# Moving the rows that GpSimd multiplies to other element offsets, and giving it 15 of 32 products

## The chip, the cores and the metric

The kernel runs on one core of one Trainium2 chip, in float32. The metric is device time in microseconds (us), the median of several executions; a separate execution was recorded by the profiler. Engines are called PE (TensorE, matmul), DVE (VectorE), ACT (ScalarE), POOL (GpSimd) and SP (SyncE, which issues the DMAs here).

## The reference, cut to what matters

The model is a conv and attention block, a position term, a Mamba stack, and a token-mixing and expert tail. The change touches only the Mamba stack: two images of 3136 tokens and 256 channels, six layers, inner width 512, 16 states per inner channel. Cut to the part around the change:

```python
def step(h, inp):
    u_t, dt_t, B_t, C_t = inp
    h = jnp.exp(dt_t[..., None] * A) * h + (dt_t * u_t)[..., None] * B_t[:, None, :]
    y_t = jnp.einsum('bds,bs->bd', h, C_t)
    return (h, y_t)
...
x_dbl = uc @ xp_w
dt_r = x_dbl[..., :DT_RANK]
Bm = x_dbl[..., DT_RANK:DT_RANK + D_STATE]
Cm = x_dbl[..., DT_RANK + D_STATE:]
dt = jax.nn.softplus(dt_r @ dt_w + dt_b)
y = selective_scan(uc, dt, A, Bm, Cm, Dp)
y = y * jax.nn.silu(z)
return y @ out_w
```

So for each inner channel and each state, a linear recurrence over the tokens: a decay exp(dt A), an input dt u B, and a product of the state with C that is summed over the 16 states.

## The kernel before, in words

The kernel has three phases in a row: `conv_phase`, `mamba_phase`, `tail_phase`. In `mamba_phase` the tokens are cut into 7 chunks of T = 448. With 2 images and 6 layers this gives 84 chunks, numbered j. The recurrence of a chunk is done in 32 scans, numbered s (i = 32 j + s over the whole phase). `order` lists them: k, one of four blocks of 128 inner channels; ng, one of four groups of states; pr, which half of the block's channels. The 128 partitions of a scan hold 32 channels for each of 4 states, and its free dimension holds two rows (g = 0, 1) of 448 tokens, for two more groups of 32 channels.

For each scan i there are these steps, each a function of its own:

- `inputs(i)`: ACT copies the kept state into element 0 of both rows of a tile x (449 elements a row). Then POOL multiplies dtur (dt u, repeated over the states) with bc row ng (B), into elements 1 to 448 (L824). The tile x comes from a pool of nine.
- `decays(i)`: ACT makes exp(dt A) in a PSUM tile da (L807, two instructions), from dtr. There are three da tiles.
- `scan(i)`: DVE runs the recurrence over 898 elements (L844). If s is in `on_pool`, it writes to x, otherwise over da, and in that case DVE at once makes the product with C (bc row 4 + ng) into x (L837 on DVE).
- `keep(i)`: ACT copies each row's last state out (L833).
- `pool_product(i)`: for s in `on_pool`, POOL makes the product with C in place in x (L837 on POOL).
- `gather(i)`, for odd i: PE sums the states of two scans into the PSUM tile acc (L859) and so frees their two x tiles. `gate(i)`, after each 8 scans: DVE multiplies acc with silu(z) (L869).
- `fetch(i)`, at the first scan of a block: SP loads the next block's dtr and dtur from DRAM (`repeat`, 8 DMAs, L781); there are two tiles of each.

B and C come from `x_keep(j)`: its result is stored to DRAM and loaded back, repeated over 32 partitions, as bc (8 rows of T elements, L625). dt and dt u come from `dt_keep`, `dt_softplus` and `dt_out(j, d)`. The last stores dt's block d, makes dtu = dt u on POOL (L652), and stores that. These and the other steps (`u_project` to `z_silu`) prepare chunk j + 1 while chunk j is scanned. The `n_` steps are the norm for chunk j + 2, and the `y_` steps the output projection of chunk j - 1.

The program is written out by hand in one order: every step is put at a place, in units of scans, all are sorted by place, and each engine runs its own instructions in that order. `places` holds the places of the preparing steps within a chunk, `first` and `last` those of steps that only some chunks have, and the loop over i those of the scan's own steps. A place fixes an order in an engine's queue, not a time; the waits between engines do the rest.

Where rows start matters to the change. Elements are counted from the start of a tile: before, bc's rows lie 448 apart, from 0; dt's and hz's rows 448 apart, from 0; dtur's rows 449 apart, from 1; the rows of x that are multiplied start at 1 and 450.

Of the kernel before, what the change touches and what calls it, by code (L numbers as in the profile page):

```python
# [10 lines left out]
F32 = mybir.dt.float32  # L11
# [7 lines left out]
P = 128  # L19
# [13 lines left out]
NB = DI // P  # L33
# [17 lines left out]
def chunk(c, n=NT):  # L51
    return slice(c * n, (c + 1) * n)
# [409 lines left out]
def mamba_phase(ctx: ExitStack, tc: tile.TileContext, I, t1_d, t2_d):  # L462
# [87 lines left out]

    M = {"dt": cp.tile([P, NB, T], F32, name="dt")}
    us = [cp.tile([P, T + 3], F32, name=f"u{n}") for n in range(2)]
    hzs = [cp.tile([P, 2 * NB, T], F32, name=f"hz{n}") for n in range(2)]
    dtus = [cp.tile([P, T], F32, name=f"dtu{n}") for n in range(2)]
# [13 lines left out]
    def u_keep(j, d):  # L570
        tail = layer_of(j + 1)["tail"][:, d, :]
        u = M["u", d] = us[d % 2]
        nc.scalar.copy(u[:, 0:3], tail)
        nc.scalar.copy(u[:, 3:], M["mm"])  # L574
        nc.scalar.copy(tail, u[:, T:])

    def u_convolve(j, d):
        ps = M["mm"] = mm()[:, :T]
        for k in range(4):
            nc.tensor.matmul(  # L580
                ps, lhsT=layer_of(j + 1)["w_cv"][:, 4 * d + k, :], rhs=M["u", d][:, k : k + T],
                start=(k == 0), stop=(k == 3),
            )
# [33 lines left out]
    def x_keep(j):  # L617

        xd = M["xd"] = one.tile([DTR + 2 * DS, T], F32, name="xd")
        nc.scalar.copy(xd, M["mm"])  # L620
        bc_d = dp.tile([2 * DS, T], F32, name="bc_d")
        nc.sync.dma_start(bc_d, xd[DTR:, :])
        bc = QS[j + 1]["bc"] = two.tile([P, 8, T], F32, name="bc")
        for n in range(4):
            nc.sync.dma_start(  # L625
                bc[chunk(n, HD)],
                bc_d.rearrange("(m n) t -> n m t", n=4)[n].unsqueeze(0).to_broadcast([HD, 8, T]),
            )
        QS[j + 1]["dt_d"], QS[j + 1]["dtu_d"] = {}, {}
# [26 lines left out]
    def dt_back(j):  # L656
        repeat(QS[j + 1], 0)
# [117 lines left out]
    def repeat(Q, k):  # L775

        dtr = dtrs[k % 2]
        dtur = two.tile([P, 4, T + 1], F32, name="dtur")[:, :, 1:]
        for t, src in ((dtr[:, :, 1:], Q["dt_d"]), (dtur, Q["dtu_d"])):
            for n in range(4):  # L780
                nc.sync.dma_start(t[chunk(n, HD)], src[k].rearrange("(g p) t -> p g t", p=HD))  # L781
        Q[k] = dtr, dtur
# [2 lines left out]
    order = [(k, ng, pr) for k in range(NB) for ng in range(4) for pr in range(2)]  # L785
    ns = len(order)

    on_pool = (2, 3, 5, 7, 8, 9, 10, 15, 19, 21, 22, 26)
    chunks = [(b, layer, c) for b in range(B) for layer in range(NL) for c in range(MCH)]
    layers, QS, X, D, acc = {}, {}, {}, {}, {}  # L790

    def layer_of(j):
        return layers[chunks[j][:2]]
# [80 lines left out]
    def fetch(i):  # L874
        repeat(QS[i // ns], i % ns // 8 + 1)
# [15 lines left out]
    def load_rest(j):  # L891
# [3 lines left out]


    places = {
        (u_project, 0): 1.304, (u_keep, 0): 2.607, (z_project, 0): 3.501, (z_keep, 0): 3.952,
        (u_project, 1): 4.609, (u_keep, 1): 5.234, (y_project, 1): 6.869, (y_add, 1): 7.331,
        (y_project, 0): 7.461, (y_add, 0): 9.223, (u_convolve, 0): 10.048, (u_add, 0): 10.687,  # L900
        (u_project, 2): 10.964, (u_keep, 2): 11.995, (u_convolve, 1): 12.277, (u_add, 1): 13.134,
        (u_convolve, 2): 14.792, (u_add, 2): 15.184, (u_project, 3): 15.393, (u_keep, 3): 16.616,
        (u_convolve, 3): 17.440, (u_add, 3): 17.991, (z_project, 1): 18.040, (u_silu,): 18.479,
        (z_keep, 1): 18.732, (x_project,): 19.334, (x_keep,): 20.167, (dt_project, 2): 20.825,
        (dt_keep, 2): 21.601, (dt_project, 0): 21.808, (dt_keep, 0): 22.204,
        (dt_project, 1): 23.295, (dt_keep, 1): 23.374, (dt_project, 3): 24.269,
        (dt_keep, 3): 24.913, (dt_softplus,): 24.942, (dt_out, 0): 25.013, (dt_back,): 25.337,
        (z_project, 2): 25.840, (dt_out, 1): 26.057, (z_keep, 2): 26.747, (z_project, 3): 27.262,
        (load,): 27.272, (dt_out, 2): 27.694, (z_keep, 3): 28.791, (n_squares,): 29.547,
        (n_root,): 29.821, (n_invert,): 31.105, (n_spread,): 32.629, (n_weighted,): 32.761,  # L910
        (load_rest,): 34.587, (dt_out, 3): 36.194, (z_silu,): 38.909,
    }
    first = {
        f_load: 12.141, f_mean: 23.145, f_center: 23.266, f_squares: 23.712, s_root: 23.835,
        s_invert: 24.267, s_spread: 25.138, f_scale: 25.476,
    }
    last = {
        l_squares: 0.000, s_root: 0.000, s_invert: 1.571, s_spread: 2.712, l_weighted: 3.271,
# [5 lines left out]
    def put(place, what, *args):  # L924
        events.append((place, len(events), what, args))
# [7 lines left out]
            put(j * ns + place, what, j)  # L933

    for i in range(n):
        put(i - 1.652, inputs, i)
        put(i - 1.217, decays, i)
        put(i + 0.4, scan, i)
        put(i + 1.080, keep, i)
        if i % ns in on_pool:  # L940
            put(i + 2.886, pool_product, i)
        if i % 2 == 1:
            put(i + 3.900, gather, i)
        if i % 8 == 7:
            put(i + 4.422, gate, i)
        if i % 8 == 0 and i % ns < ns - 8:
            put(i + 1.264, fetch, i)
    for j in range(-2, nj + 1):
        for (what, *args), place in places.items():
            target = {"y": j - 1, "n": j + 2, "l": j + 2}.get(what.__name__[0], j + 1)  # L950
# [559 lines left out]
```

## Time and profile before

| what | value |
|---|---|
| median of 3 runs | 10932.15 us (10929.53 to 10943.57) |
| the profiled execution's own time | 10941.86 us |
| its span | 10940.1 us |
| busy share of the span: PE, DVE, ACT, POOL | 82%, 88%, 70%, 81% |
| scans on DVE (L844) | 1680 into da, 1008 into x |
| products with C (L837) | 1680 on DVE, 1008 on POOL |
| inputs on POOL (L824) | 2688 |
| dt u on POOL (L652) | 336 |

The three runs lie within 14 us of each other. The page gives, for each group of equal instructions, its line, engine, operation, what it writes and reads, how many there are, then the busy time in us and the mean of one in ns, and then the idle time of that engine just before them with what ended most of it. The Mamba phase is the even middle part of the span, from about 1770 to 9600 us.

### The profile page before, as it was taken

Reading aid. Unit: us, or ns where it says so; the run is one execution under the profiler, and the core shown is the slowest. Engines: PE = TensorE matmul, PEld = TensorE weight load, DVE = VectorE, ACT = ScalarE, POOL = GpSimd, SP = SyncE. Lnnn points to the kernel's source line nnn. Section 1 sums busy time; section 2 is a strip of 40 time slices with the busy share of each in tenths; the row PEclk is TensorE's granted clock in tenths of the full one; section 3 lists DMA queues with packets and bytes.
Section 4 is the critical chain, followed back from the end, with each engine's and each line's share of the span. In section 5 each row is a group of like instructions: output and inputs, shape, how many; then the busy total and the mean of one; then the engine's idle time right before and its main releaser. Section 6 shows DMA issues by size and latency. Waiting matters only on the chain. (4 is left out here: it accounts for less than half of the span.)

```text
span 10940.1 us, 121750 instructions
## 1 busy us (share of the span) xinstructions
PE 9002.0 (82%) x39394; PEld 3541.5 (32%) x39394; DVE 9666.1 (88%) x7545; ACT 7671.5 (70%) x15776; POOL 8900.7 (81%) x5268
## 2 busy tenths in 40 slices
PE   8999997777777777777777777777777777789999
PEld 3333323323322222222332222222222222245555
DVE  6998996999999999999999999999999999967453
ACT  4664665777787777777787777778777777743343
POOL 5887996898899999999999999999999999911110
PEclk9999997888888888888888888888888888789999
DMA  1000004555555555555555555555555555511111
GB/s 48 16 16 11 16 11 97 123 128 123 117 130 120 128 121 125 120 122 128 134 140 122 127 122 122 128 121 129 121 122 123 120 125 122 127 51 31 40 40 40
DMA packets 674228, 1068.88 MB, mean 98 GB/s; under 512 B 83082, under 2 KB 668050, under 8 KB 672722
## 3 DMA queue, kind: packets, MB, share of 16 engines
q1 hardware_dynamic: 673586, 1061.09, 41.4%
q8 instruction: 309, 5.06, 0.2%
q14 instruction: 333, 2.73, 0.1%
HBM read 875.91 MB, written 184.91 MB: 97 GB/s over the span
## 5 line engine op out<-in xcount | busy, mean ns | idle before, releaser
L824 POOL TENSOR_TENSOR x<-dtur,bc 128x896 f32<-128x896 f32 x2688 | 5132.3, 1933 | 63.3 <-PE acc L859 54.5
L844 DVE TENSOR_TENSOR_SCAN da<-da,x 128x898 f32<-128x898 f32 x1680 | 3398.0, 2023 | 210.6 <-POOL x L824 145.1
L807 ACT ACTIVATE da<-dtr,am 128x449 f32<-128x449 f32 x5376 | 3428.7, 638 | 188.5 <-DVE x L844 96.6
L562 PE MATMUL mm<-xn,w_in 128*128 128x448 f32 x2656 | 1482.3, 691 | 706.9 <-ACT hz L603 238.6
L844 DVE TENSOR_TENSOR_SCAN x<-da,x 128x898 f32<-128x898 f32 x1008 | 2002.4, 2013 | 1.7 <-POOL x L824 0.9
L837 POOL TENSOR_TENSOR x<-x,bc 128x896 f32<-128x896 f32 x1008 | 1947.9, 1932 | 25.5 <-ACT state L833 17.5
L837 DVE TENSOR_TENSOR x<-da,bc 128x896 f32<-128x896 f32 x1680 | 1834.5, 1092 | 82.5 <-DVE da L844 1.8
L859 PE MATMUL acc<-x,sum_w 128*32 128x448 f32 x10752 | 1584.7, 664 | 35.6 <-POOL x L837 30.0
L335 POOL TENSOR_TENSOR pr<-kr,qo 128x980 f32<-128x980 f32 (+1 forms) x672 | 1149.0, 1722 | 196.7 <-PE pa L368 186.7
L580 PE MATMUL mm<-u,w_cv 128*128 128x448 f32 x2656 | 1089.3, 552 | 174.9 <-ACT u L574 158.2
L562 PEld LDWEIGHTS mm<-xn,w_in 128*128 128x128 f32 x2656 | 551.0, 230 | 1676.2 <-issue 733.6
L833 ACT COPY state<-da 128x2 f32<-128x2 f32 x1680 | 264.0, 157 | 1079.0 <-DVE x L837 1068.9
L360 PE MATMUL pa<-onehot,rel 49*64 49x490 f32 (+5 forms) x7168 | 834.0, 558 | 114.1 <-DVE av L377 111.4
L377 DVE TENSOR_TENSOR av<-pa,vr 128x980 f32<-128x980 f32 (+1 forms) x672 | 740.2, 1101 | 115.0 <-PE pa L368 84.9
L380 DVE TENSOR_REDUCE qo<-av 128x20 f32<-128x980 f32 (+1 forms) x672 | 743.3, 1106 | 41.4 <-DVE av L377 1.0
L309 ACT COPY vr<-vt 128x2500 f32<-128x2500 f32 (+14 forms) x296 | 468.6, 1614 | 424.6 <-DVE av L377 424.4
L580 PEld LDWEIGHTS mm<-u,w_cv 128*128 128x128 f32 x2656 | 477.3, 189 | 801.3 <-issue 372.0
L652 POOL TENSOR_TENSOR dtu<-dt,hz 128x448 f32<-128x448 f32 x336 | 382.6, 1139 | 420.3 <-ACT state L833 356.7
L368 PE MATMUL pa<-pr,hmat 64*64 64x490 f32 (+1 forms) x5376 | 641.6, 546 | 0.0
L633 PE MATMUL mm<-xd,w_dt 16*128 16x448 f32 x664 | 480.3, 814 | 186.5 <-ACT xd L620 111.1
L708 PE MATMUL mm<-hz,w_out 128*128 128x448 f32 x1344 | 553.3, 555 | 78.3 <-DVE res L715 47.4
L859 PEld LDWEIGHTS acc<-x,sum_w 128*32 128x32 f32 x10752 | 232.0, 117 | 1021.6 <-issue 819.7
(209 smaller groups left out, 11038.1 us busy)
## 6 DMA issues: line engine op xcount, KB each, us to landing
dtr<-dt_d SPq DMA_DIRECT2D x1344, 224.0 KB
dtur<-dtu_d SPq DMA_DIRECT2D x1344, 224.0 KB
bc<-bc_d SPq DMA_DIRECT2D x336, 448.0 KB
dt_d<-dt SPq DMA_DIRECT2D x336, 224.0 KB
dtu_d<-dtu SPq DMA_DIRECT2D x336, 224.0 KB
cb<-comb_d SPq DMA_DIRECT2D x128, 196.0 KB
t<-t_d SPq DMA_DIRECT2D x28, 448.0 KB
w_in<-in_in_w SPq DMA_DIRECT2D x12, 1024.0 KB
```

Source lines behind the costliest of these rows:

```text
L335: nc.gpsimd.tensor_tensor(pr[:, :, :m].rearrange("p f (q k) -> p f q k", k=KK), K[n][:, :, at : at + m].rearrange("p f (q k) -> p f q k", ...
L360: nc.tensor.matmul(pa[chunk(f, 64), g, :m], lhsT=rel[64 * g : 64 * g + rows, bh, kind, f, :], rhs=onehot[64 * g : 64 * g + rows, col : col ...
L368: nc.tensor.matmul(pa[chunk(f, 64), g, :m], lhsT=hmat[chunk(g, 64), :], rhs=pr[chunk(g, 64), f, :m], start=False, stop=True, tile_position ...
L377: nc.vector.tensor_tensor(av[:, :, :m], PA.pop(i)[:, :, :m], V[n][:, :, at : at + m], ALU.mult)
L380: nc.vector.tensor_reduce(qo[:, :, h * HW + w : h * HW + w + nq], av[:, :, :m].rearrange("p f (q k) -> p f q k", k=KK), AX.X, ALU.add,)
L562: nc.tensor.matmul(ps, lhsT=layer_of(j + 1)["w_in"][:, k, chunk(at, P)], rhs=Q["xn"][:, k, :], start=(k == 0), stop=(k == 1),)
L580: nc.tensor.matmul(ps, lhsT=layer_of(j + 1)["w_cv"][:, 4 * d + k, :], rhs=M["u", d][:, k : k + T], start=(k == 0), stop=(k == 3),)
L807: nc.scalar.activation(D[i][:, chunk(g, T + 1)], dtr[:, 2 * pr + g, :], AF.Exp, scale=L["am"][:, col : col + 1],)
L824: nc.gpsimd.tensor_tensor(x[:, :, 1:], Q[k][1][:, 2 * pr : 2 * pr + 2, :], wide(Q["bc"][:, ng, :]), ALU.mult)
L837: engine.tensor_tensor(both(X[i])[:, :, 1:], both(h)[:, :, 1:], wide(QS[j]["bc"][:, 4 + ng, :]), ALU.mult)
L844: nc.vector.tensor_tensor_scan(h, D[i], X[i], 0.0, ALU.mult, ALU.add)
L859: nc.tensor.matmul(acc[0][chunk(g, HD), :T], lhsT=sum_w, rhs=both(X[i - 1 + g // 2])[:, g % 2, 1:], start=False, stop=(ng == 3), tile_posi ...
```

## The change

The rows of bc, dt and dtur become four elements longer than T where they were T or T + 1, and the part in use begins at element 3 (bc, dt) or 1 (dtur). bc's and dt's rows then start at 3 plus a multiple of 452, dtur's at 1 plus a multiple of 452; x and hz stay as they are. The list `on_pool` grows from 12 to 15 scans of 32, and its members are others. All numbers in `places`, `first` and the loop over i are new; `last` stays.

```diff
-    M = {"dt": cp.tile([P, NB, T], F32, name="dt")}
+    M = {"dt": cp.tile([P, NB, T + 4], F32, name="dt")[:, :, 3 : T + 3]}
...
-        bc = QS[j + 1]["bc"] = two.tile([P, 8, T], F32, name="bc")
+        bc = QS[j + 1]["bc"] = two.tile([P, 8, T + 4], F32, name="bc")[:, :, 3 : T + 3]
...
-        dtur = two.tile([P, 4, T + 1], F32, name="dtur")[:, :, 1:]
+        dtur = two.tile([P, 4, T + 4], F32, name="dtur")[:, :, 1 : T + 1]
...
-    on_pool = (2, 3, 5, 7, 8, 9, 10, 15, 19, 21, 22, 26)
+    on_pool = (0, 1, 2, 5, 6, 11, 12, 13, 18, 19, 20, 21, 26, 27, 29)
...
     places = {
-        (u_project, 0): 1.304, (u_keep, 0): 2.607, (z_project, 0): 3.501, (z_keep, 0): 3.952,
...
-        (dt_keep, 3): 24.913, (dt_softplus,): 24.942, (dt_out, 0): 25.013, (dt_back,): 25.337,
...
-        (load_rest,): 34.587, (dt_out, 3): 36.194, (z_silu,): 38.909,
+        (z_project, 1): -2.539, (z_keep, 1): -2.072, (z_project, 0): -1.532, (z_keep, 0): -1.505,
...
+        (n_squares,): 15.411, (u_silu,): 16.174, (n_root,): 16.174, (n_invert,): 18.591,
...
+        (dt_softplus,): 23.997, (dt_out, 0): 24.128, (z_project, 2): 25.470, (dt_back,): 25.963,
+        (z_keep, 2): 26.109, (z_project, 3): 26.637, (load,): 26.647, (dt_out, 1): 26.808,
+        (z_keep, 3): 27.219, (z_silu,): 27.439, (dt_out, 2): 27.869, (n_spread,): 28.232,
+        (n_weighted,): 28.912, (load_rest,): 31.780, (dt_out, 3): 44.121,
     }
...
     for i in range(n):
-        put(i - 1.652, inputs, i)
-        put(i - 1.217, decays, i)
+        put(i - 3.160, inputs, i)
+        put(i - 1.850, decays, i)
         put(i + 0.4, scan, i)
-        put(i + 1.080, keep, i)
+        put(i + 0.410, keep, i)
         if i % ns in on_pool:
-            put(i + 2.886, pool_product, i)
+            put(i + 0.951, pool_product, i)
         if i % 2 == 1:
-            put(i + 3.900, gather, i)
+            put(i + 3.316, gather, i)
         if i % 8 == 7:
-            put(i + 4.422, gate, i)
+            put(i + 4.228, gate, i)
         if i % 8 == 0 and i % ns < ns - 8:
-            put(i + 1.264, fetch, i)
+            put(i + 0.050, fetch, i)
```

More of the change, by code (lines that the diff above doesn't have):

```diff
@@ L897, in mamba_phase @@
     places = {
-        (u_project, 0): 1.304, (u_keep, 0): 2.607, (z_project, 0): 3.501, (z_keep, 0): 3.952,
[L899 to L903, printed above, removed]
@@ L904, in mamba_phase @@
-        (z_keep, 1): 18.732, (x_project,): 19.334, (x_keep,): 20.167, (dt_project, 2): 20.825,
-        (dt_keep, 2): 21.601, (dt_project, 0): 21.808, (dt_keep, 0): 22.204,
-        (dt_project, 1): 23.295, (dt_keep, 1): 23.374, (dt_project, 3): 24.269,
-        (dt_keep, 3): 24.913, (dt_softplus,): 24.942, (dt_out, 0): 25.013, (dt_back,): 25.337,
-        (z_project, 2): 25.840, (dt_out, 1): 26.057, (z_keep, 2): 26.747, (z_project, 3): 27.262,
-        (load,): 27.272, (dt_out, 2): 27.694, (z_keep, 3): 28.791, (n_squares,): 29.547,
@@ L910, in mamba_phase @@
-        (n_root,): 29.821, (n_invert,): 31.105, (n_spread,): 32.629, (n_weighted,): 32.761,
-        (load_rest,): 34.587, (dt_out, 3): 36.194, (z_silu,): 38.909,
+        (z_project, 1): -2.539, (z_keep, 1): -2.072, (z_project, 0): -1.532, (z_keep, 0): -1.505,
+        (u_project, 0): -1.249, (u_keep, 0): -0.200, (u_project, 1): 1.151, (u_keep, 1): 1.663,
+        (y_project, 0): 4.063, (y_add, 0): 5.160, (y_project, 1): 5.762, (y_add, 1): 6.434,
+        (u_convolve, 0): 7.637, (u_add, 0): 7.892, (u_convolve, 1): 8.295, (u_add, 1): 8.658,
@@ new lines, in mamba_phase @@
+        (u_project, 3): 9.800, (u_keep, 3): 10.138, (u_project, 2): 11.100, (u_keep, 2): 11.358,
+        (u_convolve, 3): 13.166, (u_add, 3): 14.088, (u_convolve, 2): 14.814, (u_add, 2): 15.199,
+        (n_squares,): 15.411, (u_silu,): 16.174, (n_root,): 16.174, (n_invert,): 18.591,
+        (x_project,): 19.692, (x_keep,): 19.881, (dt_project, 0): 20.231, (dt_keep, 0): 20.575,
+        (dt_project, 2): 21.356, (dt_keep, 2): 21.523, (dt_project, 3): 22.720,
+        (dt_keep, 3): 23.054, (dt_project, 1): 23.113, (dt_keep, 1): 23.784,
@@ L912, in mamba_phase @@
+        (dt_softplus,): 23.997, (dt_out, 0): 24.128, (z_project, 2): 25.470, (dt_back,): 25.963,
+        (z_keep, 2): 26.109, (z_project, 3): 26.637, (load,): 26.647, (dt_out, 1): 26.808,
+        (z_keep, 3): 27.219, (z_silu,): 27.439, (dt_out, 2): 27.869, (n_spread,): 28.232,
+        (n_weighted,): 28.912, (load_rest,): 31.780, (dt_out, 3): 44.121,
     }
     first = {
-        f_load: 12.141, f_mean: 23.145, f_center: 23.266, f_squares: 23.712, s_root: 23.835,
-        s_invert: 24.267, s_spread: 25.138, f_scale: 25.476,
+        f_load: 2.954, f_mean: 5.165, f_center: 5.401, f_squares: 6.561, s_root: 7.195,
@@ L916, in mamba_phase @@
+        s_invert: 9.457, s_spread: 10.252, f_scale: 10.610,
     }
```

## The prediction, made before the changed kernel was run

> **What bounds the kernel now.** The page's slices came first: from about 1770 to 9600 us VectorE and GpSimd both stand at 9 tenths, TensorE at 7. This is the Mamba stage, 84 chunks of 32 scans; nothing outside it is edited. I then asked for the busy times of an even stretch (columns: length, busy time and count of PE, PEld, DVE, ACT, POOL, then clock, DMA share, GB/s):
>
> ```profile
> 2650.00:9200.00 6550.00, 5130.30 (x18392) 1861.30 (x18396) 6252.26 (x4340) 5148.02 (x11974) 6199.20 (x3424) 0.84 0.54 125
> ```
>
> and for the groups by line of the same stretch, first VectorE, then GpSimd:
>
> ```profile
> L844 DVE TENSOR_TENSOR_SCAN da<-da,x 128x898 f32<-128x898 f32 x1410 | 2851.9, 2023 | 181.0 <-POOL x L824 124.2 <-ACT da L807 56.0
> L844 DVE TENSOR_TENSOR_SCAN x<-da,x 128x898 f32<-128x898 f32 x848 | 1684.3, 2013 | 0.0
> L837 DVE TENSOR_TENSOR x<-da,bc 128x896 f32<-128x896 f32 x1410 | 1539.7, 1092 | 70.2 <-DVE da L844 1.8 <-PE mm L580 1.4
> ```
>
> ```profile
> L824 POOL TENSOR_TENSOR x<-dtur,bc 128x896 f32<-128x896 f32 x2257 | 4309.6, 1933 | 44.4 <-PE acc L859 43.9
> L837 POOL TENSOR_TENSOR x<-x,bc 128x896 f32<-128x896 f32 x849 | 1640.8, 1933 | 23.0 <-ACT state L833 15.4
> L652 POOL TENSOR_TENSOR dtu<-dt,hz 128x448 f32<-128x448 f32 x280 | 319.0, 1139 | 282.2 <-ACT state L833 268.4 <-PE mm L562 13.8
> ```
>
> The scans number 1410 + 848 = 2258, so the stretch holds 2258 / 32 = 70.56 chunks of 92.83 us. In each, VectorE works 6252.3 / 70.56 = 88.6 us and idles 4.2; GpSimd works 87.9 and idles 5.0, of which 4.0 ahead of L652, waiting for dt. VectorE waits most for GpSimd's inputs (124.2 us). The two are a matched pair: neither can be relieved by loading the other unless that other becomes faster. ScalarE works 73.0 us a chunk and TensorE 72.7; neither is the bound.
>
> **What a removed VectorE product saves.** Instructions overlap a little, so I take steps from start to start, from the timeline of VectorE (start, length, instructions, how many in a row):
>
> ```profile
> 5056.24 3.94 DVE L844 TENSOR_TENSOR_SCAN x<-da,x 128x898 f32<-128x898 f32 x2
> ...
> 5060.61 2.03 DVE L844 TENSOR_TENSOR_SCAN da<-da,x 128x898 f32<-128x898 f32 x1
> 5062.67 1.09 DVE L837 TENSOR_TENSOR x<-da,bc 128x896 f32<-128x896 f32 x1
> 5063.68 2.02 DVE L844 TENSOR_TENSOR_SCAN x<-da,x 128x898 f32<-128x898 f32 x1
> ```
>
> A scan with VectorE's product steps 5063.68 - 5060.61 = 3.07 us. One whose product is GpSimd's steps 3.94 - 2.01 = 1.93. Each moved product saves 1.14 us; 12 to 15 saves 3.4 us a chunk, leaving VectorE 85.2.
>
> **What a GpSimd product will cost** decides everything: at today's cost it can't take three more. Its steps now, from its timeline:
>
> ```profile
> 5044.44 11.35 POOL L824 TENSOR_TENSOR x<-dtur,bc 128x896 f32<-128x896 f32 x6
> ...
> 5060.80 1.93 POOL L824 TENSOR_TENSOR x<-dtur,bc 128x896 f32<-128x896 f32 x1
> 5062.68 1.94 POOL L837 TENSOR_TENSOR x<-x,bc 128x896 f32<-128x896 f32 x1
> ```
>
> Six in 11.35 us is (11.35 - 1.93) / 5 = 1.885 a step: 0.046 under the duration. Does the distance of the operands matter? These groups of GpSimd, over the whole execution with shapes apart, say that something does:
>
> ```profile
> L335 POOL TENSOR_TENSOR pr<-kr,qo 128x980 f32<-128x980 f32 x448 | 813.5, 1833 | 163.1 <-PE pa L368 153.3 <-DVE xo L253 1.1 <-DVE qo L380 0.5
> L652 POOL TENSOR_TENSOR dtu<-dt,hz 128x448 f32<-128x448 f32 x336 | 382.6, 1139 | 420.3 <-ACT state L833 356.7 <-ACT dt L644 48.8 <-PE mm L562 13.8
> L335 POOL TENSOR_TENSOR pr<-kr,qo 128x784 f32<-128x784 f32 x224 | 336.0, 1500 | 33.6 <-PE pa L368 33.4
> ...
> L1087 POOL TENSOR_TENSOR x<-x,g 128x784 f32<-128x784 f32 x16 | 29.6, 1853 | 181.0 <-DMA g<-gate_d 166.9 <-ACT r L1030 14.1
> ...
> L236 POOL TENSOR_TENSOR xo<-xo,pe_in 128x896 f32<-128x896 f32 x14 | 29.3, 2094 | 0.0
> ```
>
> L652, L1087 and L236 read two operands at distance 0 (rows of 448 or 392 and whole tiles, all multiples of four). From 448 to 896 elements they go from 1139 to 2094 ns: 2.13 ns an element and 185 fixed. Two rows in one instruction cost nothing extra: L1087 has two of 392, and the line gives 1855. L335, whose second operand stands still for 49 elements, takes (1833 - 1500) / 196 = 1.70 an element. So 1.70 is the rate without the second stream's advance, 2.13 with both in step. The Mamba products, at 1933, lie between: (1933 - 185) / 896 = 1.95.
>
> Why between? Before, dtur's rows lie 449 apart from element 1, and bc's rows at 0. One product therefore holds rows at distances 1 and 2 (pr = 0) or 3 and 4 (pr = 1); L837's rows of x lie at 1 and 2. If distance counts modulo four, 4 is 0, and pr = 1 gives distance 3 directly: 2 x 1.95 - 2.13 = 1.77, near the bare 1.70. Then pr = 0 must have one slow row and one fast (1 and 2 sum to 3.90 too). Of these I take 2 as fast: it is farther from coincidence than 3, so should be no slower, and then 1 must be the slow one. After the change L824 has distance 2 in all rows (1 less 3), L837 has 2 and 3, L652 has 3. Product: 185 + 896 x 1.77 = 1.77 us, step 1.725; L652: 185 + 448 x 1.77 = 0.98, step 0.935. Bounds: 1.70 gives 1.71, and no effect leaves 1.93; a distance worse than 0 is shown nowhere, so 2.09 is the top. I take 1.77, with the two sums agreeing to a few ns across all groups.
>
> GpSimd a chunk: 47 x 1.725 + 4 x 0.935 + 0.3 (rest) = 85.1 us, against VectorE's 85.2. Matched again, 3 us lower.
>
> [...]
>
> **The remaining edits.** bc, dt and dtur get four more elements a row. The DMAs keep their counts and 1792 byte rows; dtr's rows already begin one element in. dt_softplus reads rows instead of one run: nothing to 0.2 us on ScalarE, which has 20 us free. VectorE's 17 products read bc from element 3: nothing, at most 0.01 us each, as its rows read at 0, 1 and 2 alike.
>
> New places: every order changes, but the close relations stay: pool_product(i) still follows inputs(i+4); decays(i) still follow keep(i-3). The state copy ahead of inputs(i) moves from after keep(i-3) to after keep(i-4), so GpSimd may lead by one more scan. That helps VectorE's 1.8 us a chunk of waits for it. Against that, an x tile lives from i-3.16 to its gather at i+3.3 or i+4.3: of nine tiles 1.5 to 2.5 slots are spare, where 2.4 to 3.4 were (L824's 43.9 us wait for acc is this). u_silu and n_root become neighbours, one table load (1283 ns) of ScalarE less. dt_out(3) moves to 44.121, behind inputs(15) in GpSimd's queue and just ahead of fetch in SP's: SP stands there for dtu, and the loads queue behind. Store and loads need some 13 us (a fetch ran from 5004.75 to 5014.6); GpSimd has 8 inputs and 4 products, 12 x 1.725 = 21 us, before inputs(24) needs them. Covered; without cover the difference would be idle of GpSimd.
>
> I keep the idle at 4.2: more lead, against less slack between the pair (0.1 us, where it was 0.7). Chunk: 85.2 + 4.2 = 89.4, so 84 x 3.4 = 286 us less. The profiled execution took 10941.9 (span 10940.1), 10 over the median: 10656, or about 10645 by the median.
>
> **Rivals.** (1) Products get fast but the tighter pair idles 1.7 us more a chunk, on x tiles or order: 84 x 1.7 = 143 us given back, 10790 (10700 to 10900). (2) Slower: there is no period of four; only exact coincidence is slow, so 1 to 4 all cost 1.95. It explains pr = 0 and pr = 1 being equal just as well. GpSimd then needs 47 x 1.885 + 4 x 1.01 + 0.3 = 92.9; with the 1.0 us of its idle that isn't L652's it makes 93.9, plus 90 us: 11020; with all 5.0, 11360. It decides from a mean product over 1.83 us (all idle kept) to 1.91 (1.0 kept). (3) Also slower: even distances slow, odd fast. pr = 0 and 1 fit this too. L824 becomes 2.09 (step 2.04), L837 stays 1.93: 65.3 + 28.3 + 3.7 + 0.3 = 97.6, plus 1.0: 11420, at worst 11750.
>
> **Chances.** Forecast 0.66, own range 10520 to 10760; rival 1 0.10; no change 0.03 (0.2%, 22 us, is what a measurement of this kernel can tell); rival 2 0.13; rival 3 0.08. Smoothness with distance speaks against 3, the nearness of 1.77 to 1.70 against 2. Faster 0.76, same 0.03, slower 0.21. The low end takes half of the 2.6 us that VectorE idles for inputs and decays, some 110 us more; the high end, 10950, reaches rival 1 and no change, and leaves out rivals 2 and 3.
>
> **What would show it.** Right: L824 and L837 on GpSimd at 1.75 to 1.80, L652 near 0.98, 1260 products with C there and 1428 on VectorE, VectorE's idle near 4 us a chunk, chunks of 89 to 90. L824 still 1.93 is rival 2, 2.09 with L837 1.93 rival 3; fast products with GpSimd waiting for acc is rival 1. The forecast is wrong if L824 stays above 1.83.

## The result, and the profile after

The changed kernel takes 10975.26 us (median of 6 runs, 10965.17 to 10979.45) against 10942.42 for the kernel before in the same runs: a ratio of 1.0030, 95% interval 1.0019 to 1.0041. It is slower by 0.3%, where 2.6% less was predicted. The profiled execution has a span of 10973.8 us. One of the four executions of `after_warm`, below, was in a slower state (12159.67 us at a mean granted clock of 0.68), so its time here is the median of the other three, 10745.23 us; expectations that say 10750, 10751 or 224 us count all four.

The same even stretch (columns: length, busy time and count of PE, PEld, DVE, ACT, POOL, then clock, DMA share, GB/s):

```profile
2650.00:9200.00 6550.00, 5220.88 (x18345) 1903.96 (x18344) 6018.38 (x4121) 5072.00 (x11868) 6015.32 (x3625) 0.85 0.55 124
```

The groups by line there, VectorE, then GpSimd:

```profile
L844 DVE TENSOR_TENSOR_SCAN da<-da,x 128x898 f32<-128x898 f32 x1196 | 2418.8, 2022 | 40.7 <-ACT da L807 39.1 <-ACT x L823 0.9 <-ACT state L833 0.4
L844 DVE TENSOR_TENSOR_SCAN x<-da,x 128x898 f32<-128x898 f32 x1056 | 2087.4, 2013 | 303.7 <-ACT state L833 263.8 <-ACT da L807 39.8
```

```profile
L824 POOL TENSOR_TENSOR x<-dtur,bc 128x896 f32<-128x896 f32 x2252 | 3947.2, 1771 | 137.0 <-PE acc L859 134.9 <-DMA dtu_d<-dtu 1.0 <-PE mm L562 0.5
L837 POOL TENSOR_TENSOR x<-x,bc 128x896 f32<-128x896 f32 x1055 | 1872.6, 1775 | 258.8 <-ACT state L833 258.8
L652 POOL TENSOR_TENSOR dtu<-dt,hz 128x448 f32<-128x448 f32 x280 | 273.8, 978 | 91.9 <-ACT dt L644 90.7
```

The work came out as costed: products 1771 and 1775 ns, L652 978 ns. With 1196 + 1056 = 2252 scans the stretch holds 70.4 chunks of 93.07 us, so VectorE works 85.5 us a chunk (3.1 less than before) and GpSimd also 85.5 (2.4 less). But VectorE idles 7.55 us a chunk instead of 4.22. What it waits for (us in total, times, longest):

```profile
DVE x L844 <- ACT state L833: 263.8, 135, 3.9
DVE res L715 <- PE mm L708: 75.7, 55, 3.4
DVE x L844 <- ACT da L807: 39.8, 29, 2.5
DVE da L844 <- ACT da L807: 39.1, 59, 1.2
DVE xn L690 <- DMA vec<-in_mamba_vec: 30.5, 10, 4.8
```

The waits for GpSimd's inputs, 124.2 us before, are gone. In their place the scans wait for ScalarE, 342.7 us or 4.9 a chunk. The name L833 misleads; the timelines of ScalarE and VectorE over one such wait show for what:

```profile
5617.98 0.63 ACT L639 ACTIVATE dt<-mm,vec 128x448 f32<-128x448 f32 x1 [1.34 <-PE mm L633]
5618.51 1.30 ACT L807 ACTIVATE da<-dtr,am 128x449 f32<-128x449 f32 x2
5619.75 0.15 ACT L833 COPY state<-da 128x2 f32<-128x2 f32 x1
5620.56 0.63 ACT L639 ACTIVATE dt<-mm,vec 128x448 f32<-128x448 f32 x1 [0.65 <-PE mm L633]
...
5621.29 1.28 ACT L644 ACT_TABLE_LOAD   x1
5622.59 1.70 ACT L644 ACTIVATE dt<-dt 128x1792 f32<-128x1792 f32 x1
5624.31 1.28 ACT L807 ACT_TABLE_LOAD   x1
5625.60 1.31 ACT L807 ACTIVATE da<-dtr,am 128x449 f32<-128x449 f32 x2
```

```profile
5622.55 1.09 DVE L837 TENSOR_TENSOR x<-da,bc 128x896 f32<-128x896 f32 x1
5627.02 2.03 DVE L844 TENSOR_TENSOR_SCAN x<-da,x 128x898 f32<-128x898 f32 x1 [3.37 <-ACT state L833]
```

The decays end at 5625.60 + 1.31 = 5626.91 and scan 26 starts at 5627.02. Ahead of them ScalarE ran one piece without decays (a table load, ACT_TABLE_LOAD in the trace, takes 1283 ns; in the stretch one stands ahead of each of the 70 `dt_softplus`, 70 `u_silu`, 70 `z_silu` and 83 roots, 213 at the return to decays and 10 at a new layer's `am`, L535): the last `dt_keep`, a table load, `dt_softplus`, the load back. It began late because `dt_keep` had twice stood for TensorE (1.34 and 0.65 us). Summed by scan over the trace, VectorE idles 2.87 us a chunk ahead of scan 26, 1.07 ahead of 19 (behind `u_silu` with `n_root`), 0.57 ahead of 30 (behind `z_silu`), 0.56 in slot 29, nearly all of it in `n_weighted` (L690), and about 1.08 in slot 7, where `y_add` (L715) waits for its projection. Slot s is the time from the end of scan s - 1 to the start of scan s.

### The profile page after: what moved, and what is told of

It is laid out like the page before. It is cut to its first block, busy times and chain, and to the rows that moved or that the text cites. A ratio compares the mean times of both kernels' runs of the same rounds, so it can differ in the third digit from the quotient of the medians.

```text
span 10973.8 us, 121652 instructions
## 1 busy us (share of the span) xinstructions
PE 9140.9 (83%) x39394; PEld 3594.4 (33%) x39394; DVE 9403.1 (86%) x7293; ACT 7604.4 (69%) x15693; POOL 8700.6 (79%) x5520
## 5 line engine op out<-in xcount | busy, mean ns | idle before, releaser
L824 POOL TENSOR_TENSOR x<-dtur,bc 128x896 f32<-128x896 f32 x2688 | 4711.7, 1771 | 214.3 <-PE acc L859 203.2
L844 DVE TENSOR_TENSOR_SCAN da<-da,x 128x898 f32<-128x898 f32 x1428 | 2887.9, 2022 | 53.0 <-ACT da L807 46.6
L844 DVE TENSOR_TENSOR_SCAN x<-da,x 128x898 f32<-128x898 f32 x1260 | 2491.4, 2013 | 382.4 <-ACT state L833 308.7
L837 POOL TENSOR_TENSOR x<-x,bc 128x896 f32<-128x896 f32 x1260 | 2236.6, 1775 | 310.3 <-ACT state L833 310.3
L562 PE MATMUL mm<-xn,w_in 128*128 128x448 f32 x2656 | 1384.3, 651 | 462.3 <-ACT hz L603 376.5
L859 PE MATMUL acc<-x,sum_w 128*32 128x448 f32 x10752 | 1647.8, 680 | 43.2 <-POOL x L837 41.8
L837 DVE TENSOR_TENSOR x<-da,bc 128x896 f32<-128x896 f32 x1428 | 1558.8, 1092 | 61.3 <-PE acc L859 0.5
L562 PEld LDWEIGHTS mm<-xn,w_in 128*128 128x128 f32 x2656 | 529.0, 222 | 1369.1 <-ACT hz L603 564.0
L708 PE MATMUL mm<-hz,w_out 128*128 128x448 f32 x1344 | 658.0, 642 | 314.5 <-DVE res L715 199.2
L833 ACT COPY state<-da 128x2 f32<-128x2 f32 x1428 | 225.9, 158 | 846.4 <-DVE x L837 841.7
L633 PE MATMUL mm<-xd,w_dt 16*128 16x448 f32 x664 | 517.1, 872 | 257.8 <-ACT xd L620 194.5
L859 PEld LDWEIGHTS acc<-x,sum_w 128*32 128x32 f32 x10752 | 260.7, 120 | 1095.2 <-issue 747.4
L666 PE MATMUL mm<-mb_mean_w,sq 128*112 128x1 f32 x1728 | 284.7, 295 | 284.6 <-ACT sq L662 283.8
```

The source lines that it names most:

```text
L562: nc.tensor.matmul(ps, lhsT=layer_of(j + 1)["w_in"][:, k, chunk(at, P)], rhs=Q["xn"][:, k, :], start=(k == 0), stop=(k == 1),)
L824: nc.gpsimd.tensor_tensor(x[:, :, 1:], Q[k][1][:, 2 * pr : 2 * pr + 2, :], wide(Q["bc"][:, ng, :]), ALU.mult)
L837: engine.tensor_tensor(both(X[i])[:, :, 1:], both(h)[:, :, 1:], wide(QS[j]["bc"][:, 4 + ng, :]), ALU.mult)
L844: nc.vector.tensor_tensor_scan(h, D[i], X[i], 0.0, ALU.mult, ALU.add)
L859: nc.tensor.matmul(acc[0][chunk(g, HD), :T], lhsT=sum_w, rhs=both(X[i - 1 + g // 2])[:, g % 2, 1:], start=False, stop=(ng == 3), tile_posi ...
```

## The experiments

The theories named in the expectations: A, ScalarE's pieces of table loads and functions hold up the decays; B, GpSimd's own queue does; C, TensorE's clock is halved where dt is projected, so dt is late. Work and idle are VectorE's, in us a chunk over the stretch from 2650 to 9200 us; ratios are to the kernel before in runs beside each (medians 10940 to 10951 us), so a difference between kernels of different groups of runs carries some 10 us of that.

| kernel | median us | ratio (95%) | work | idle |
|---|---|---|---|---|
| before | 10942.42 | | 88.6 | 4.22 |
| the change | 10975.26 | 1.0030 (1.0019 to 1.0041) | 85.5 | 7.55 |
| rows_only | 10903.12 | 0.9963 (0.9953 to 0.9974) | 88.6 | 3.68 |
| order_only | 11045.17 | 1.0089 (1.0074 to 1.0105) | 85.6 | 8.58 |
| rows_pool15 | 11000.79 | 1.0051 (1.0035 to 1.0066) | 85.8 | 7.85 |
| after_one_table | 10525.36 | 0.9612 (0.9596 to 0.9628) | 85.2 | 2.82 |
| before_one_table | 10728.53 | 0.9795 (0.9780 to 0.9809) | 88.5 | 1.89 |
| after_warm | 10745.23 | 0.9814 (0.9798 to 0.9831) | 85.5 | 4.93 |
| before_warm | 10794.19 | 0.9858 (0.9845 to 0.9872) | 88.7 | 2.62 |
| rows_only_warm | 10775.38 | 0.9840 (0.9827 to 0.9854) | 88.5 | 2.51 |
| replan | 10858.67 | 0.9915 (0.9900 to 0.9930) | 85.7 | 6.16 |
| replan_warm | 10844.37 | 0.9901 (0.9884 to 0.9917) | 85.6 | 5.86 |
| after_warm_split | 10903.63 | 0.9956 (0.9943 to 0.9970) | 85.7 | 6.57 |
| after_warm_split2 | 10907.15 | 0.9968 (0.9956 to 0.9980) | 85.6 | 6.65 |
| spread_warm | 10920.66 | 0.9978 (0.9969 to 0.9986) | 85.5 | 6.97 |
| cleared_warm | 10801.74 | 0.9867 (0.9852 to 0.9882) | 85.5 | 5.60 |
| spread | 11034.62 | 1.0083 (1.0069 to 1.0097) | 85.5 | 8.19 |
| cleared | 11023.69 | 1.0071 (1.0059 to 1.0084) | 85.6 | 8.04 |
| late_blocks | 10817.94 | 0.9891 (0.9877 to 0.9905) | 85.5 | 5.91 |
| late_blocks_warm_8 | 10711.56 | 0.9792 (0.9779 to 0.9806) | 85.3 | 4.69 |

The work column hardly moves among the kernels with 15 products; the times follow the idle column.

**The parts of the change.** rows_only is the kernel before with the three tiles' new rows; order_only has the new list and places on the old rows; rows_pool15 has the new rows and list on the old places.

> The kernel before with the new rows alone (old places, 12 products on GpSimd). Both theories: L824 and L837 on GpSimd at 1.77 us, L652 at 0.98, VectorE's work unchanged at 88.6 us a chunk. Theory A (in the changed kernel the stalls come from ScalarE's blocks of table loads and functions, which its new order sets against runs of short scans): the waits of VectorE for GpSimd's inputs (1.8 us a chunk) go, little else changes: 10780 to 10830. Rival B (in the changed kernel the stalls come from GpSimd's own queue, x tiles and kept states, and would do so at this speed in any order): no gain, 10930.

> The changed kernel with the old rows: new places, 15 products on GpSimd, at 1.93 us each. GpSimd needs 47 x 1.885 + 4 x 1.094 + 0.3 = 93.3 us a chunk and becomes the bound. Theory A: its idle shrinks to about 1 to 3 us, as ScalarE's blocks then hide behind GpSimd: 94.5 to 96.5 a chunk, 11080 to 11250. Rival B: its present idle of 7.6 us a chunk stays, as it lies in its own queue: 100.9 a chunk, 11620.

> The kernel before with the new rows and the new list of 15 scans, but all old places. VectorE's work 85.2 us a chunk, GpSimd's 85.1. If the places are what lost the gain (both theories), idle stays at 4 to 5 us and the time is 10640 to 10720. If the list itself (four scans of 1.93 us in a row, 18 to 21) loses it, idle is 7 us or more and the time 10870 or more.

GpSimd's groups over the stretch, first of rows_only, then of order_only:

```profile
L824 POOL TENSOR_TENSOR x<-dtur,bc 128x896 f32<-128x896 f32 x2271 | 3973.2, 1771 | 83.9 <-PE acc L859 80.3 <-DMA dt_d<-dt 1.8 <-DMA dtu_d<-dtu 1.1
L837 POOL TENSOR_TENSOR x<-x,bc 128x896 f32<-128x896 f32 x852 | 1511.7, 1774 | 439.0 <-ACT state L833 438.2
```

```profile
L824 POOL TENSOR_TENSOR x<-dtur,bc 128x896 f32<-128x896 f32 x2225 | 4259.4, 1938 | 6.7 <-PE acc L859 6.6
```

The rows alone make every product fast. GpSimd gains 7.5 us a chunk and the time falls by only some 40 us, since VectorE, unchanged, is now alone the bound; that lies between what A and B expected. Fifteen products on old rows are slower, as GpSimd then has 93.3 us of work a chunk, though less slow than either theory said. The third run is the telling one: with fast products, the new list costs 98 us on the old places too. Its largest wait of VectorE over the stretch:

```profile
DVE x L844 <- ACT da L807: 180.7, 69, 2.7
```

That is scan 20, behind `u_silu`: VectorE idles 0.85 us a chunk ahead of it in rows_only and 2.67 here, with the same places. So it is not some slip in the new places alone; taking these products off VectorE lengthens its idle in either order.

**ScalarE's tables.** Edit, in the Mamba stage of both kernels: Silu, Softplus and Sqrt are replaced by Exp, so that these functions are left out and the table loads around them with them (516 in the stretch of the change, 7.3 a chunk, none in that of after_one_table).

> The changed kernel with Exp in place of Silu, Softplus and Sqrt in the Mamba phase, which changes those functions and so takes nearly all of ScalarE's table loads away (about 6.5 of 1.283 us a chunk), and nothing else. Theory A: VectorE's idle falls from 7.5 us a chunk to 3 or 4.5: 10590 to 10720. Rival B: the waits of GpSimd for acc and for kept states stay and so does VectorE's idle, over 6.5 us: 10890 or more.

> The control for the run with one table: the kernel before with Exp in place of Silu, Softplus and Sqrt in the Mamba phase, which changes those functions and takes nearly all table loads away (8.5 of 1.283 us a chunk on ScalarE), nothing else. Theory A (ScalarE's blocks cost far more in the changed kernel's order than in the old one): VectorE's idle falls only from 4.2 to about 2.5 us, as GpSimd at 87.9 us of work is close to the bound: 91 us a chunk, 10770 to 10850, a gain of 100 to 180 where the changed kernel gained 450. Rival (the table loads cost about as much in any order): a gain near 400, 10550.

The changed kernel's idle falls by 4.73 us a chunk, to 2.82; that of the kernel before by 2.33. With ScalarE out of the way the change is worth 10728.53 - 10525.36 = 203 us. ScalarE is where the lost gain went, though by busy time it has 21 us a chunk free (5072.0 of 6550.0 us are busy). Both came out faster than A expected. (Both runs also lighten ScalarE by some 10 us of busy time a chunk, so they show the engine, not yet which piece.)

**TensorE's clock.** The last matmuls of dt's projection, in the profile of the changed kernel, windows of TensorE first (columns as above: the clock stands after POOL), then its timeline:

```profile
5610.00:5615.00 5.00, 5.00 (x16) 1.03 (x20) 4.96 (x4) 2.52 (x8) 5.00 (x4) 0.55 0.41 93
5615.00:5620.00 5.00, 4.28 (x12) 0.99 (x4) 4.93 (x4) 3.50 (x10) 5.00 (x4) 0.50 1.08 205
```

```profile
5612.65 1.85 PE L633 MATMUL mm<-xd,w_dt 16*128 16x448 f32 x2
5614.43 1.72 PE L859 MATMUL acc<-x,sum_w 128*32 128x448 f32 x8
```

TensorE is busy for all of the first window, at a clock of 0.55, and for 4.28 us of the second, at 0.50. Most of what runs there is small beside the 128*128 of L854 or L562: L633 uses 16 rows, L859 32 columns. The edit pads L633's contraction with zeros to 128 rows and leaves its result as it is:

```diff
+    xd_full = cp.tile([P, T], F32, name="xd")
+    nc.gpsimd.memset(xd_full, 0.0)
+    w_dt_full = cp.tile([P, DI], F32, name="w_dt")
+    nc.gpsimd.memset(w_dt_full, 0.0)
...
-            ps, lhsT=layer_of(j + 1)["w_dt"][:, chunk(d, P)], rhs=M["xd"][:DTR, :],
+            ps, lhsT=layer_of(j + 1)["w_dt"][:, chunk(d, P)], rhs=M["xd"],
```

> The changed kernel, where dt's projection contracts over 128 rows in place of 16 (the rows added are zero, and so is what they add): same matmuls, same number of passes, same order. Theory C (TensorE's clock falls to half in the stretch of dt_project since its matmuls fill an eighth of the array, this delays dt_keep on ScalarE and with it the decays ahead of slot 26): the granted clock in that stretch rises to 1.0, ScalarE's waits at L639 (265 us in the stretch) halve, VectorE's idle falls from 7.6 us a chunk to 5 to 6.5: 10780 to 10890. Rival (the clock has another cause, or dt_keep's lateness doesn't matter): clock and time as before, 10970.

> The kernel before, with the contraction of dt's projection (L633) padded from 16 to 128 rows by zeros, as in the run after_warm. Theory C (the half clock of TensorE in slots 21 to 25 makes dt late, and dt holds up ScalarE and then the scans): in the kernel before, VectorE idles 1.74 us ahead of the scan in slot 27, waiting for an input whose dt u came late, and ScalarE waits 188.7 us for L633 in the stretch from 2650 to 9200 us. Both shrink; up to 84 x 1.7 = 143 us less: 10800 (10780 to 10870), less than the 224 us that the same edit took off the changed kernel, so that the change itself, once dt is on time, is worth 50 to 100 us. Rival: the zero rows help both kernels alike (some 220 us, 10720), and the change then is worth nothing even with the clock at full speed.

> The kernel before with the new rows alone (12 products with C on GpSimd and the old places), and the zero rows of after_warm. Theory C: of the 3.70 us a chunk that VectorE still idles with the new rows, the 1.06 ahead of the scan in slot 27 goes, so 84 x 1.0 = 85 us less than rows_only's 10903: 10815 (10790 to 10850). The longer list and the new places are then worth 60 us of their own on top (after_warm 10751). Rival (the longer list earns nothing, the clock is all): rows_only_warm comes out at or below after_warm's 10751.

The same places in after_warm, windows and timeline (five lines were added above, so L633 is L638 and L859 is L864):

```profile
5595.00:5600.00 5.00, 4.40 (x22) 1.29 (x22) 4.96 (x4) 4.50 (x14) 5.00 (x4) 1.00 0.42 104
5600.00:5605.00 5.00, 2.94 (x12) 0.74 (x8) 4.97 (x4) 3.84 (x11) 5.00 (x4) 1.00 1.08 202
```

```profile
5598.19 1.02 PE L638 MATMUL mm<-xd,w_dt 128*128 128x448 f32 x2
5599.14 0.96 PE L864 MATMUL acc<-x,sum_w 128*32 128x448 f32 x8
```

TensorE is now less busy and at full clock, and the pair of matmuls takes 1.02 us instead of 1.85. Just ahead of these matmuls TensorE idles for the same time in both (2.41 and 2.39 us), and the first pair behind that pause takes 1.01 and 1.02 us, so that pause alone does not halve the clock. The same shows over the stretch: the mean of one matmul falls from 866 ns to 626, ScalarE's wait for them at `dt_keep` from 265.4 us to 112.7, and the idle ahead of scan 26 from 2.87 us a chunk to 0.73. Against the change, 230 us are gone, more than C expected, and a kernel with 15 products beats the kernel before. But before_warm takes 148 us off the kernel before too: the half clock was there already (0.59 and 0.50 from 5015 to 5020 and to 5025 us in the trace of before, at dt's projection), and it cost less there. Of VectorE's waits for GpSimd's inputs, 124.2 us before, this is left in before_warm:

```profile
DVE da L849 <- POOL x L829: 7.9, 13, 0.9
```

They had been nearly all at one place, scan 27, whose input waited for a late dt u: 1.71 us a chunk, and 0.10 with the zero rows, although GpSimd's products are as slow as before (the mean of its instructions in the stretch is 6311.17 / 3484 = 1.811 us there, and 6199.20 / 3424 = 1.811 before). With the clock up in all three, the rows are worth 10794 - 10775 = 19 us and the list with its places some 30 more. VectorE's idle is still 2.4 us a chunk higher with the change (4.93 against 2.51). So C is a cause, and not the whole.

**Other places, and shorter pieces.** replan has another list (2, 3, 5, 6, 7, 10, 11, 12, 14, 19, 20, 21, 22, 27, 28) and other numbers for every place, among them

```diff
-        (dt_softplus,): 23.997, ... (z_silu,): 27.439,
+        (dt_softplus,): 24.833, ... (z_silu,): 28.469,
...
-        put(i - 1.850, decays, i)
+        put(i - 1.930, decays, i)
```

and replan_warm adds the zero rows.

> The changed kernel's rows and 15 products, with places and a list of scans chosen anew, by hand counting in which ScalarE's table loads block its queue and TensorE's matmuls of few rows run at half clock. Theory A: VectorE's work of 85.4 us a chunk stays and its idle falls to 2 to 4.5 us: 10480 to 10690. Rival B (15 products can't pay in any order, as x tiles and kept states bind): 10850 or more.

> The kernel replan, with dt's projection over 128 rows as in after_warm. Theory C: 0 to 100 us less than replan, as its order leaves room for the half clock already; rival (the clock doesn't follow the rows in use): equal to replan within 10 us.

The rows and 15 products stay, list and places go, and 117 us go with them. That misses A's range, and lies in B's; but after_warm shows 15 products paying, so B's reason is out. The zero rows then bring only 14 us more, though ScalarE's wait for dt's projection falls from 181.1 us to 29.7: here late dt hardly counted. So what the clock costs depends on list and places. The next two cut ScalarE's longest piece in after_warm, first by moving `n_root`, then `n_invert` as well:

```diff
-(u_silu,): 16.174, (n_root,): 16.174, (n_invert,): 18.591
+(u_silu,): 16.174, (n_root,): 17.600, (n_invert,): 22.000
```

> after_warm with n_root at place 17.600 instead of 16.174, so that u_silu and n_root are no longer neighbours. In after_warm, ScalarE runs a table load, u_silu, a table load, n_root and the load back in one piece of about 6 us, and VectorE idles 1.08 us a chunk ahead of the scan in slot 19, waiting for decays behind that piece. Theory A (what is left of the lost gain is the length of such pieces): cut in two, of 4.3 and 2.8 us, they no longer outlast the lead of the decays, although ScalarE gets one table load more (2.6 us a chunk): slot 19's idle nearly goes, 60 to 90 us less, 10670 (10655 to 10700). Rival: ScalarE's sum counts, not the piece; the additional load makes later decays late instead, and the time stays at 10750 or rises to 10800.

> after_warm_split with n_invert (the reciprocal on VectorE that waits for n_root) at place 22.000 instead of 18.591. In after_warm_split, VectorE stood 1.77 us a chunk at n_invert, since n_root had been put behind u_silu and a pair of decays while n_invert kept its place in VectorE's queue. Theory A (the length of one piece of ScalarE's work without decays is what stalls the scans): with n_invert out of the way the two shorter pieces no longer stop VectorE, slot 19's idle falls from 1.75 (1.08 in after_warm) to at most 0.4, and the time comes out 50 to 100 us below after_warm's 10751: 10670 (10650 to 10710). Rival (ScalarE's sum counts: one table load there and back more, 2.6 us a chunk, makes later decays late): 10751 or above, up to 10850, with the wait moved to slots 20 to 26.

Both cost over 150 us, more than even the rivals allowed. VectorE's waits in the first and in the second:

```profile
DVE rsn L681 <- ACT rsn L678: 125.8, 71, 3.0
```

```profile
DVE x L849 <- ACT da L812: 175.1, 94, 2.5
```

In the first VectorE stands at `n_invert` in its own queue. In the second that wait is gone, and VectorE idles 2.03 us a chunk ahead of scan 20 instead. ScalarE's timeline there, from `u_silu`'s load to the decays of scan 20:

```profile
5769.19 1.28 ACT L602 ACT_TABLE_LOAD   x1
...
5773.63 1.31 ACT L812 ACTIVATE da<-dtr,am 128x449 f32<-128x449 f32 x2
...
5775.05 1.28 ACT L678 ACT_TABLE_LOAD   x1
...
5778.01 1.31 ACT L812 ACTIVATE da<-dtr,am 128x449 f32<-128x449 f32 x2
```

Between the two pieces stand the decays of one scan only, scan 19: in 5778.01 - 5769.19 = 8.8 us ScalarE makes no others, and of the scans that VectorE runs meanwhile 18 and 19 are GpSimd's, short ones. Cutting a piece in two helped nothing where its parts stayed that close.

**The list.** Theory D: the moved products shorten VectorE's steps, and rows of GpSimd's scans leave ScalarE no time to catch up. spread has on_pool = 1, 3, ..., 29; cleared has 0, 2, 4, 6, 8, 10, 12, 13, 15, 16, 20, 22, 23, 27, 31; each also with the zero rows.

> after_warm with on_pool = 1, 3, 5, ..., 29: still 15 of 32 products with C on GpSimd, none next to another; places as they are. Theory D (ScalarE can't catch up in a row of GpSimd scans: VectorE's step there is 1.93 us, ScalarE's own part of a scan 1.42, so 0.5 us a scan is left for other work, against 1.65 where VectorE makes the product): alternating, two scans leave 2.15 us, everywhere alike, and the stalls at slots 19 and 26 (1.08 and 0.74 us a chunk) shrink to a half or less; VectorE's idle from 4.93 to 2.5 to 4: 10750 - 84 x 1.0 to 2.4 = 10600 (10550 to 10680). Rival A (the pieces of ScalarE's work outlast the lead of the decays, wherever the products are made): idle stays 4.5 to 5.5: 10750 (10700 to 10800).

> after_warm with on_pool = 0, 2, 4, 6, 8, 10, 12, 13, 15, 16, 20, 22, 23, 27, 31: 15 products again, but the scans 17 to 19, 24 to 26 and 28 to 30, which run while ScalarE does u_silu with n_root, dt_softplus and z_silu, all keep VectorE's product and so the long step. Theory D: those pieces cost 5.8, 4.3 and 4.3 us, and three long scans leave 3 x 1.65 = 5.0 us beside the lead of the decays; idle ahead of the scans there falls under 0.3 us each, below spread_warm: 10560 (10520 to 10650). Rival A: as after_warm, 10750 (10700 to 10800). A second rival: GpSimd gets 10 of its products within slots 0 to 16, falls behind there, and VectorE waits for inputs instead: 10700 and more, with the wait for L829.

> The changed kernel (no zero rows) with on_pool = 1, 3, 5, ..., 29. Theory D with C: the clock still halves in slots 21 to 25 and dt comes late, but ScalarE makes up for it, since no row of GpSimd scans follows: idle from 7.57 to 3.5 to 5.5: 10975 - 84 x 2 to 4 = 10720 (10640 to 10810). Rival (the clock alone made the changed kernel slower): idle stays within 1 us of 7.57: 10900 to 11050.

> The changed kernel (no zero rows) with on_pool = 0, 2, 4, 6, 8, 10, 12, 13, 15, 16, 20, 22, 23, 27, 31. Theory D with C: the block of dt_softplus still comes late by the half clock, but it falls on the long scans 24 to 26: 10700 (10600 to 10800). Rival (the clock alone): 10900 to 11050.

D failed. All four are slower than the same kernel with the list of the change. (Their rival for the kernels without zero rows, the clock alone, falls with late_blocks below, which has no zero rows either.) Scans 19 and 26 stall under every list: scan 19 by 1.34 to 1.40 us a chunk, scan 26 by 4.05 in spread, 3.36 in cleared, 2.84 and 1.23 with the zero rows. Where VectorE stalls goes with the places; how long depends on the list too. One trait of D is left: in spread scan 25 is GpSimd's, so the two scans beside the piece before scan 26 are 3.07 - 1.93 = 1.14 us shorter than in the change, and scan 26 idles 4.05 - 2.87 = 1.18 longer.

**The place of a piece within a scan.** ScalarE's order in the kernel before, at the same steps:

```profile
5022.95 0.64 ACT L639 ACTIVATE dt<-mm,vec 128x448 f32<-128x448 f32 x1 [1.30 <-PE mm L633]
5023.48 1.30 ACT L807 ACTIVATE da<-dtr,am 128x449 f32<-128x449 f32 x2
5024.73 0.15 ACT L833 COPY state<-da 128x2 f32<-128x2 f32 x1
...
5024.91 1.31 ACT L807 ACTIVATE da<-dtr,am 128x449 f32<-128x449 f32 x2
5026.16 0.62 ACT L639 ACTIVATE dt<-mm,vec 128x448 f32<-128x448 f32 x1
5026.79 1.28 ACT L644 ACT_TABLE_LOAD   x1
```

Two scans' decays stand between the last two `dt_keep`, and the last waits for nothing. In the change it was one, and ScalarE stood 0.65 us. The places say so: before, `dt_softplus` (24.942) came after decays(26) (24.783) and keep(23); in the change (23.997) it comes after decays(25) (23.150) and keep(23) (23.410). `z_silu` lost one scan's decays in the same way. late_blocks gives them back in the changed kernel (the first `dt_out` moves along), and moves nothing else:

```diff
-(dt_keep, 1): 23.784, (dt_softplus,): 23.997, (dt_out, 0): 24.128, ... (z_silu,): 27.439
+(dt_keep, 1): 24.160, (dt_softplus,): 24.170, (dt_out, 0): 24.250, ... (z_silu,): 28.200
```

late_blocks_warm_8 adds the zero rows, and takes scan 18 off `on_pool` for scan 8.

> The changed kernel with four places moved by a fraction of a scan: dt_keep of block 1 from 23.784 to 24.160, dt_softplus from 23.997 to 24.170, dt_out(0) from 24.128 to 24.250, z_silu from 27.439 to 28.200. In ScalarE's queue the two pieces with table loads then stand behind decays(26) and decays(30), and ahead of keep(24) and keep(28). Theory F: three scans' decays are done when such a piece starts, instead of two, and the wait of dt_keep for TensorE (1.3 us at the last one) is spent on decays(26). The idle ahead of scans 26, 29 and 30 (2.87 + 0.56 + 0.57 us a chunk) shrinks by 1.9 to 2.4, some coming back ahead of scan 27: 10975 - 84 x 1.9 to 2.4 = 10790 (10740 to 10850). Rival A: a piece displaces the same work of ScalarE wherever it stands, the idle moves to scans 27 and 31 in full: 10975 (10940 to 11000).

> late_blocks with the zero rows of after_warm, and with scan 8 in on_pool instead of scan 18. While ScalarE does u_silu and n_root (16.174), VectorE runs the scans 16, 17 and 18; with 18's product on VectorE they last 3 x 3.07 us instead of 8.07. Theory F: after_warm idles 4.93 us a chunk; of this 1.0 ahead of scans 29 and 30 goes by the place of z_silu, up to 0.7 ahead of scan 26, and 0.9 to 1.08 ahead of scan 19 by the list: 10751 - 84 x 1.9 to 2.7 = 10560 (10525 to 10620). Rival A: as after_warm, 10750 (10720 to 10780); with the list alone working, 10670.

ScalarE's timeline in late_blocks, and VectorE's wait over the stretch:

```profile
5539.43 1.30 ACT L807 ACTIVATE da<-dtr,am 128x449 f32<-128x449 f32 x2
...
5540.86 1.31 ACT L807 ACTIVATE da<-dtr,am 128x449 f32<-128x449 f32 x2
5542.10 0.61 ACT L639 ACTIVATE dt<-mm,vec 128x448 f32<-128x448 f32 x1
5542.74 1.28 ACT L644 ACT_TABLE_LOAD   x1
```

```profile
DVE x L844 <- ACT state L833: 121.0, 120, 1.4
```

The order of before is back, and the lost time with it, as theory F expected: 157 us less than the change, for four numbers, with the same work. The idle ahead of scan 26 falls from 2.87 to 0.10, and 1.02 comes back in slot 27. These two make up the whole gain: slot 7 (`y_add`) idles 0.85 less as well, but slots 1, 2 and 29 to 31 take that back. `z_silu`'s move gained next to nothing: its idle went from scan 30 (0.57) to scan 31 (0.50). Slot 29 was not its doing: L690 waits there, for a new layer's weights (51.9 us in 10 waits of the stretch, in the chunks that open a layer, where it was 30.5) and for its own matmuls. The last kernel is the fastest that leaves nothing out, 2.1% under the kernel before; scan 19 waits 0.29 instead of 1.08. It missed its expected time by 150 us. VectorE's longest waits there:

```profile
DVE xn L695 <- DMA vec<-in_mamba_vec: 48.2, 10, 5.9
DVE x L849 <- ACT da L812: 44.7, 22, 2.5
DVE xn L695 <- PE mm L687: 43.5, 54, 1.5
```

L695 is L690's line there, in slot 29. The expectation had put that slot's idle down to `z_silu`.

## Why the prediction was wrong

- **The saving and GpSimd's cost: right.** L824, L837 and L652 came out at 1771, 1775 and 978 ns against 1.77 us and 0.98; the period of four, argued from two sums, agrees with these three groups, with rows_only's (1771, 1774, 979 ns) and with order_only's on the old rows (1938, 1937, 1143). That distance 2 is fast, and not 1, was a choice with little behind it; L824, now at 2 in all rows, bears it out. VectorE works 85.5 us where 85.2 was said, some 25 us over 84 chunks. Rivals 2 and 3 (no period, or even distances slow) are out, and rows_only shows this without list or places. VectorE's waits for inputs went, as hoped. But "a matched pair" went too far: those 124.2 us were mostly late dt at scan 27, and before_warm takes them away with GpSimd's products as slow as before. `dt_out(3)` was covered, as said: GpSimd waits 1.2 us for DMAs ahead of L824 over the stretch. (Counted from the span's start, as everywhere here, the fetch that the prediction puts at 5004.75 to 5014.6 runs from 4993.52 to about 5003.4.)
- **"I keep the idle at 4.2": the step that failed.** It measured 7.55: 3.35 x 84 = 281 us, more than the 3.1 x 84 = 260 that the products had saved. Rival 1 had the right form ("x tiles or order") at half the size, 1.7 us; no rival had fast products and a slower kernel. Of its two causes it was the order; x tiles made GpSimd wait (134.9 us for acc), while none of VectorE's larger waits is for GpSimd.
- **Why it failed.** "Neither is the bound" was read from ScalarE's mean of 73.0 us a chunk. Its decays can lead by three scans at most, the da tiles, and a piece with table loads takes that lead. And the idle was carried over as if it were a property of the kernel: a VectorE that is 3.1 us quicker reaches the same pieces sooner, and meets whatever was hidden. rows_pool15 shows this on the old places (scan 20), and after_one_table what it is worth.
- **"The close relations stay": true only among a scan's own steps.** I compared decays(i) with keep(i-3), and not with the preparing steps that share ScalarE's queue. Working out for `dt_softplus` which decays are ahead of it would have shown three before and two after. late_blocks puts 157 us on it.
- **"One table load ... less" was named as a gain alone.** The counts did fall, but the merged piece of `u_silu` and `n_root` is longer, and scan 19 idles 1.07 us a chunk behind it.
- **TensorE's 72.7 us was taken as harmless.** The page's clock row stood at 8 tenths and was not asked where. A clock of 0.50 to 0.55 at dt's projection makes `dt_keep` late (265.4 us of waits over the stretch, 112.7 with the zero rows); the zero rows took 230 us off the change and 148 off the kernel before.
- **What the wait for TensorE and for weights adds.** `y_add` waits 75.7 us over the stretch, and L690 30.5 for a new layer's weights; neither wait was there before. The new places put `n_weighted` closer to its load (28.912 against 26.647, before 32.761 against 27.272), which is the likely reason. Neither was costed; what each is worth alone was not tried.

The shares do not add up, since late dt and a misplaced piece meet at the same scan. With the clock up and the pieces back, the change still idles 2 us a chunk more than the kernel before with the clock up (4.69 against 2.62). The traces show where: `n_weighted` waits 1.26 us a chunk against 0.38, `y_add` 0.49 against nothing, and slots 2 and 31 idle 0.80 and 0.51 against under 0.1 each, while the 0.86 ahead of scan 20 in before_warm is gone. What mending each would give stays open.

## What to carry to other kernels

Work taken off the busiest engine is a gain only as far as the others can follow at each point of the order, so cost the idle as carefully as the work: for every piece of an engine with ample mean slack, count how many of the next steps are done when it starts. Where an order is made anew, compare each preparing step with the steps it is queued among, not those steps with each other. And ask the profile where the granted clock is low before calling TensorE free.

## What the runs showed of the hardware

- GpSimd's two-operand products in float32 ran at 1.77 ns an element (beside 185 ns fixed) where the first operand's start less the second's was 2 or 3 elements modulo four, as against 2.13 at distance 0 (before: L652 1139 ns for 448 elements, L236 2094 for 896); rows at distances 1 and 2, or 3 and 4, gave the mean (1933 ns for 896 elements). The 1.77 stands for 1771 ns of L824 (distance 2), 1775 of L837 (2 and 3) and 978 of L652 (3, 448 elements). That 1 is a slow one, and that the count goes modulo four, is inferred from those sums.
- TensorE's granted clock was 0.55 and 0.50 in two windows of 5 us in a row in which it was busy for 5.00 and 4.28 us, mostly with matmuls that used 16 of 128 rows or 32 of 128 columns: 1.85 us for two of the first kind over 448 tokens. With rows of zeros added the same two took 1.02 us at a clock of 1.00; over the stretch the mean of one fell from 866 to 626 ns. In the kernel before it was 820 ns, and the zeros raised the mean clock of the stretch from 0.84 to 0.88. Whether the 32 columns count too was not tried. Those zeros were the largest gain of any edit here that leaves the computation whole.
